# A mixture-of-experts and selective-scan block on one core: expert rooms of 184, 336, 200 and 380 slots, and a job order found with other durations

## The chip, the cores and the metric

The kernel runs on one core of one Trainium2 chip. The metric is device time in microseconds of that core, from start to end of one execution. The core has five engines with programs of their own: PE (TensorE, matrix products and transposes), DVE (VectorE), ACT (ScalarE), POOL (GpSimd) and SP (SyncE, which here issues transfers). Transfers are carried out by 16 DMA engines.

## The reference

The input x has 16×256 tokens of 128 numbers, 4096 tokens in all. Four parts follow each other, each on a layernorm of x and each added to x:

```python
x = x + attn_a(layernorm(x))   # softmax rows sum to 1: in effect one linear map, v then w_out
x = x + ffn(layernorm(x))      # 8 experts, top 2 of a softmax gate
x = x + attn_b(layernorm(x))   # selective scan, 16 states, decaying sums along 256 tokens
x = x + ffn(layernorm(x))      # the same experts once more
...
logits = x @ gate_w;  top_vals, top_idx = top_k(logits, 2);  w = softmax(top_vals)
h = relu(x @ w1[e])            # 128 -> 512
y = h @ w2[e]                  # 512 -> 128
out = sum over the two experts of w * y
```

The reference runs all tokens through all experts and weighs with zeros; the kernel sends a token only to its two experts.

## The kernel before

**Tiling.** The tokens are cut into 8 blocks of 512. Each of the two expert layers treats blocks in sets: `FIRST` (layer 1) is [0], [1], [2,3], [4,5], [6,7]; `SECOND` (layer 2) is [0,1], [2,3], [4,5], [6], [7]. Layer 1 of a set is followed by the scan mixer of its blocks (`arrive`, `mixer`), and layer 2 by the output (`finish`).

**Routing.** For a set, `route` finds each token's two experts and its place in the expert's room, scales the row by the gate's weight, and scatters it to a buffer `slots` in device memory with indirect transfers issued by POOL (4 per block and choice, 128 in all). `experts` then goes over the 8 experts. `collect` gathers each token's two result rows from `ys` (128 indirect transfers of POOL) and adds them to x.

**Rooms.** `SLOTS` gives the slots per expert: its first tuple is for layer 1, its second for layer 2, and within each the first number is for sets of one block and the second for sets of two. `divided` rounds a room to nc chunks of np partitions: nc is the room over 128, rounded up, and np the room over nc, rounded up. So 192 is 2×96, 330 is 3×110, 216 is 2×108 and 384 is 3×128. If an expert gets more tokens than its room, a flag that is read at the end runs the whole of `general()`.

**One expert pass** (`experts`, N slots as C chunks of K partitions): a fetch `xs<-slots` (SP, K partitions × C rows of 512 bytes, strided in device memory by the 8 experts), C transposes on PE, an eviction `xsT`, four products with `w1` (128×N each), relu into `h`, four products with `w2` into `ps_y`, an eviction `yT`, C transposes, an eviction `yr`, and a store `ys<-yr` on SP. There are 80 passes, and so 80 fetches and 80 stores: 16 passes of 192 slots, 24 of 330, 24 of 384, 16 of 216. The tiles xs and yr have four buffers each. The fetch and the store are

```python
x = new("xs", [P, CMAX, P], bufs=XS)[0:K, 0:C]
move(x, q.part(q.slots, e, i), 4 * N * P, turn="fetch")
...
move(q.part(q.ys, e, i), yr, 4 * N * P, key=f"out{q.name}")
...
v = t[NE * i * self.n : NE * (i + 1) * self.n]
return v.rearrange("(p c e) w -> e p c w", e=NE, c=self.nc)[e]
```

**The mixer** treats a block in 8 steps of two states each. A step has two pairs of PE products that spread the states' rows over partitions (`ps_B`, `ps_C`), exponentials and tanh on ACT, and on DVE a product, a scan of 1024 elements (`w`) and two more products; pairs of steps are added (`th`, on DVE or POOL) and go through PE into `ps_s`.

**What sets the order.** Nothing is issued while the program is written down: every operation becomes a job of `Plan` with a duration from `cost` (line 712; matmuls in line 780, transfers in `move`), the tiles it needs and the jobs it follows. `forward` builds a schedule: it takes, again and again, the job that can start earliest, and among equals the one with the better rank; jobs that `either` lists with several engines (PSUM evictions, some additions) go to the one that starts first. The ranks are decoded from the string `ORDER`. The program is then written in order of these starts, so that each engine's program, SP's and POOL's among them, is fixed; on the chip each engine runs its program in that order. All jobs are recorded under line 710 of the profile; scatters are line 807, gathers line 821.

Of the kernel before, what the change touches and what calls it, by code (L numbers as in the profile page):

```python
# [40 lines left out]
XN, ROW, XS, XT, H, YT, DEPTH = 4, 3, 4, 3, 4, 3, 3  # L41

ORDER = (
    "c-oy;3zS?{m92a3_kHWtzxw}AcS6!hI-~;z$O;57;6V8Q2_u0S5d^_uSc)<WMU9}iM3yW-9GO9x!6gH;R9KFnMgszpL;?f?f"
    "k*<R^Xq@t@4Y*x(n)u9Rdv$gbywAU_uY5jJ?HGR&pu3!7%XbbZAPKv1@3dL7-PWr9y>~ce89&%(C@K%Jo9!(hVu?i`7ck&TU"
    "=}!eF%Vl)_8eOGlzoV+GCP40*uyj))&`!j{^V`L0}L96gZ<4gs;O)2b>A*3(6>rA1qHftKE)g1PD&+d4C53zj>tYtuRmST4)"
    "&WZ=i;-Wdt8&k}Jkz4frZfW0dx>2F9<qDP7bBq>YMzaZlQu8;l;?+ePSH#x<oKoEc04YdQ9_z#2UcR8YkQZ@_JKUIwrXpCBw"
    "y%n$|z+H*Fet87`^C*_nH1fcC_oYqiEa5-i%s&Llw`v@46X#t7>ItB=v6B`tD>z8D<E*H}0f-#>loAIJY14hsV+|<5QxV>F6"
    ">MACb|KehA*xQaiirRK`r;~{cLjneDt0Nf|kEoo*U@p9_j!i#dWsezvrR+sxshv)zuWsGhFh-7pml~U+|6RMg#e{BnBi1OJ8"
    "{AtKz1A~GTIhQXQRn%ke_1+;3-()<bWZJRR6xkpvtH^UoJyCT1TFBd-vKZw{l=N5^8I7n;k;oMd;@Ct0ds)?$Q&UmPXz}F6#"  # L50
    "dW9?-*SWOvxor10@uUMTT|4)h($^?t#9+p%<8@UwC4u_H&;{uTgXsAMiMbl@4dSA0RXZ4ACKM^vhG!qIZ3nF^_^|>`d-Tn&K"
    "wyzk<LlLQRB1Sh~zY_bopU;AF}%AS(s#+{Wm8iwK;{49U2`nGz1AY|+UEUrmJ%G;LyF9NZ`WH88wyQ>luGWVmKT3OV<!#{EW"
    "z!NIr5>A!W@A}UR$AWI|yFk+BEncN=R!(&QNPwlz&?wY>(L5$Xj@WkfMZ5@g#l8cWfdX#yell3CZhJqETdv4Sl?uKS~-)v})"
    "*4Vd22ckBKk|8VVy=0BLVS=}uE1S@ZYfgCSgm>u8<lgqPqc<;kc?rNJurWMKMhvbR2qEm+|2UcJKs<96Vvpuj0d3D4Ol{~jD"
    "cbd9cbIWM858=Cz7YhCRBII%{;(YO>*0hKYgrutqLc+%P%RBi3%*?jzD0>I3<3Efd@<bwI+I<3KauaD-H2gE37^e)@TEs7Rl"
    "mCTe(M@e{Hq2=o>!CxJnq#en9mpN*lS+&Iw2j!+`ts4{f2PVMHH#yYYq^BZsi=|-|t8(JfC6;{iqKJpA{YQK>8{db}Y7%1%m"
    "$WPD1#pR5Rju3=MF*JyEdPx|=W?&I655)808;G9f7ezWWA3XfwvOg@aHMUvd&5l5TnkS>p^$u;L$4aYP5jbo}#ADG_H0DKuj"
    "u!Z7tjkurLfov96nM^nzTX@8{Q$937vRW0C-5uOb^Oj3%l#B4<#!j~c5E#e_fwC;J+RCpwK|NPft1JPleU~<FVRNIdf6eaz_"
    "Nv0P>Z+A!CEICH}&6*u~1??PyUf7eg8@uY%b;<r%k|>f-k1T$sZg1Me)YxXVdWNeW?%8tuHdp{3#ogBbYA;w0bivzZvubm=S"
    ";u|tWYNdXxF6B#=HHK)3%~O5?RK;+SsOX+qgTI%sagY#bZ33c{lh?fXeo(UeK9XlQ!l>}&R7jB33OpT{afUf*+^D_6L!6*c<"  # L60
    "h7L9m@!!-^s_fy|QfmDvDt?3h}Vp{*$OLDcCS%nsc8svmPfsu)&;TDFcKF;EU}a@<8*34~xXDg|A}%sHpKTeo9dE`>kiXNE!"
    "2}Rao~0CdHr>Vh5vv;!0oyH0!d8k45OvgXmyL7+J<Yl^FG(U|O>XL3Z^p+mWlK0Gj2vl>bFE98-Xh<|d<ttXm_ycw_46$d*="
    "N{H*TW<G$1MvHzy|X*oCAKl|_DUET4E2{EZ~6~SV(+hdkJ2eiw&E}+CZo)u}D7<-j8X)h}#*5`2TRY(d%ak`I(om3YX7XQ;-"
    "82r-(aOFxjFT(DFH3&d<{WUmyg<*(gK;*T8E51PH6`c5O%$++arQY0k=N}_YL3^ZMXC|Hk8Tkp7kug{EMoc)KVA>SNEd*jOR"
    "9YC!pixRCZz|TuC8>TjE2Sd2j>|k}_jex`*77FX%xVN5;iP64HL+aT94Q(>1jRGe9_6W#Uzmtbw}b7x^s&|tS_9HVKCt5A<r"
    ";K3#2~{Q$LJJ~Hs`_xjttq@*ZSwWyjf2SC@AZj@tRoMK)SD!2#kI>vgzGf`??{<_J?ayD>|GN-@g6sACYC`O>cGby6Yag{&{"
    "i}+$XP#SP|(-qF~Kw%fXLgv}ls@Vcf(y{7%z2MX{bU?!9o?c~7re&u%04nm5av&iTz*iXBTg#+qYc$6S5>Z_diGZg@Lf6Z@l"
    ")wW4G;Y_;oS5sUq}{^J@BankP?#tvB!n0-i|(&S41wf@8QeqzI@v|6^xKn>E_@SbQwN(5yWll87$l4ZQ+dV~^R$DnXlPzYRo"
    ")nh#23O4sr7AdIyNKVav-OU8V&iXsz8B^JL-v%twpAwQ=Qp|pL-T}0+fY4v3M`J_Ct2}NOAeM^U#$*H;)v^arT5v56Py~LZy"
    "KtG#Z#A8=wV{w6{Aq2UK4;F$;&&I4XD{lhb2fGEE&R*a#-{EVssn+QktixhOrgXABzgXo6auRe$x$=KXq4BsUH~Xp{8b1kln"  # L70
    "N+6lChLhmik8mt@M}Y;tMZR#K=n$X_u5IpFss8+P{mW+v!LiI0f_TD5d!MEHHWJ{fMhI2>AeM8WT~lFC&MDJMTtfyM<#FVQG"
    "6lvYlzEg5Xy?ijwILJC0%|7jEaAdM4HQ9Ul^>ZtxO2d*7_vQ`_~SaB^+CfzpN?51RLemBMwz*BO@dmSRRDbMiV)Q)90R8v)z"
    "PHZ9pW?~U#))Iqb7HGfO(OYbK0V2jtFoI3HtT9vb*jfliR`xD_|=fpUst#pJqUfuD|?7`1i9dy4PmcQ6C_ua2TI`NL#X@*mg"
    "FRefEuh)`e$Qz<7@yzC)%_k#wz7<VN(?nT?jN!h38#$$@B&A}fNhKD)_V3C>6?W_Km;UG4d2i226s4(^Prc~oj9DzqGETcK8"
    "l1I%Z`po^mmqr`!`l4Z+3U}RBpKnhl}a~$D~2#N!gR!o$meVKHLX;2^h2XY87cFhMkAv)*fxxquK9mk7i_+QICRJ`ksSbxqM"
    "*I8qi^KK9B8|S>`kad*b*wWhc}`O7B-;)d)e~yQKVGI!z@(HG(2T0$>Pb^WShXEOR;`2lv#Y9kQb>_Ogj2i=fq_yU67CeVZr"
    "{@gsGEVbJj_oU$d>DPTCh!;?-g}h~-P|d6M0v5E0K_4$xYQ1gxnot`W$KR~PH@`L`l|7UC;<sTQxWUQ6||poTy22!i!IhKzy"
    "pXQf3l-Gg!A-@Dv~rsY^rO)gVE@UZZmD)VdP0}msHuac5QY{JGYJL#qvpHEjmiedOSa1F&HY|ulVc)O@cHts`I{@eiBjwR(!"
    "_8ix^k!l0(h~&T7vM4e5KVN*DYOK3E+dhbWdb3?O^7)&A1eAW?=7Vz!2K8hi*_g1DL}BPd81oY)3j%rzwa6$#het4-Ihzya7"
    "77H$j6raj9Caxc6jsy)rla2BZ#kLR!ussM?-TivyE_K=-%6eQ%Dy}IKPmF8KGQE(BPY{&sD0aUkypJowK$5&pz3Zxld!;r4b"  # L80
    "i{@8#QJ_IFn*;{VzcdLVpURg@j=$V-dy;p8g9$&<0E*5r}RnW4ssP!0vkwhv!q5M?mqtJQ-&7z$ANdJr>3`CNU5J!(3K065A"
    "i+L-$}&JeEnTAef=kA}-sw&-e>J#HChX&52<yMomPBiDcydpfxkF<esn+mybj<nYg@AEfou;>8oatI$$gl&*zUTVA&_w=>d0"
    ")VuxalN-e>{1?hHd#T<gEY603Sq;ya#Gqh_Mm3NVtcv12paWEAp@N;jl_QKli;?LCjg<s`!{TB$IU6ISyA=LpWVI7x57}ZFu"
    "UyR@ii5A&vj>Y+kR=nMcOp1blceu7K&ZmLJKbnmXE#R8F_*sih9<z#X+;A%6{A{Ez$^$XzqzsgPamGSd;v$zQUxv|TBU}pJO"
    "amc?{~0On8j*%t>`(S5uz_(gF0ig2eO`~@C)l`YfsL7i$mXvUPy{QQMzyN>t{N*$*BV(<B)RH{Zi?qJ-47zZD6A6QTNl6PX5"
    "ISpC}NRp5Pnd{WL_F(JZ&*EA26kJwh%tbQBz`jL{MqK*a1OmW2Y&=;)dCIpY+M<9hn6WW0SGk%=for-_rsND|HXUrYeDY^Wt"
    "uRc9iXm1sqF%8mqwdiz%BgB3yFq0D1xK{)d$SD=|z!!`R#$kn*RmVr&^uNvVT^94rO$#9JszL!=M5ANyV03eex*#vqAJ5%Ny"
    "4jqAju=(&N=4uCL$VU#40LZNbPG?#1NILG;DwkqZqSz2uCi;rN@$1`Lu><|JJbQm8p-oY1<G0KV!2gME%*-8+W+2sVI7iO}V"
    "by#4#`*ZG+D5_>`9E(B_QH4OGPsRbTmB)28Dj{m%J|AhKbS}aVhfpCwQ3T%8MPLEt0_hZ!m=-&iwY`GPJ764^K~`KA)|>;ZT"
    "@}ro$BSFRTs>(OgIUG3@gF-FYys&tR|0K7L5=Q1R;Acpqk2X^1mlt)<4r;#9V#Ar;xBaY8bA8LwH`k|bnD=W9={Cqp~?6mho"  # L90
    "&4_Wy<Nnt3%6`4o`d?Jc7`~W)6IU(A0xWeYE66moHm&C{%Swf1)8>zM4L0V)e(guDC4q`lQj5u0A+aaZ8un3Qd1Ymv1sxdPR"
    "bXpF`2ny4=hvZmZ(jB1TFvQ!y*3d@871G&uZwjyQCLcvtak_0a06QK|H{u2@M=iF$eXLNf~A_>t8mIX5}CBwCXxTAHI}2I<h"
    "`E~}xkx}PS^I0)w{z$;7M(mMgE@bH1*P=z1LhC|cMJ}fL|GOVkadMHZ|Iwe#A`toNgp%6N%#M5OoJ7Xx|oBi^Al<r1{j)cBY"
    "l~?L1sL<2Fxe}N<G+K_!DGWB1<tAJ`9fwY^rJe?ox=L6Hjs_FgT9+F+bp=uascEUaWHugt_1Qsn0t`Y``6H-EgwhO|E(3LFi"
    "Z?4fSLUZ9QdC9!r$s_l{2aE7_!YHqVmIU{%F`z!%!=I%kKZ5%&Cmzc%b~}~q>IM!rb81tqy!K!VUCYqq#7$!!==bhCX=3s;$"
    "%^*;wCa3OO-O9o(ZQ-hqNQio)L;mia^O(WxDCmOmSION~THP!{KuJTjQtx^z2P$M2bgM$Pd4pP-rZqEAXmI7_yZA^bv5zLiv"
    "(<9@0~Uc6m5-C3WfQIGd(iPb1aJH#rlw)TN|RU9cU3796-NOrQ-8{Em$WuY$d&)W2z2U6(ZvewlXCrKM0GRTY^=ugp-!=%Y&"
    "Fsu8My`l0<!hGyKW_?@eYMLo3~SMyobTC68?dK%$h)m{3q^-@n)MyH}zA67bsj(WIKz)be3x{NFe<qcAG^{A`%9Fy8f&&*3R"
# [1408 lines left out]
```

## Time and profile before

| | |
|---|---|
| median of 9 runs | 724.56 us (719.81 to 727.77) |
| profiled execution, its own time | 724.92 us |
| its span | 723.2 us |
| mean granted clock of PE | 0.916 |
| busy: PE / DVE / ACT / POOL | 624.1 / 554.4 / 487.9 / 414.7 us |
| first expert matmul / first scan | 50 / 128.4 us |
| expert matmuls of 192 slots | 57 to 131 us |
| of 330 slots | 137 to 388 us |
| of 384 slots | 398 to 638.9 us |
| of 216 slots | 641.6 to 698.2 us |
| last scan ends | 622.7 us |

The profile is of one execution. Busy time is given per engine, and a matmul in four-byte floats appears as two records. "PEclk" is the clock that was granted to PE, as a share of its full speed. Windows give, for a stretch of time, the busy time of each engine in it (with the number of instructions), the granted clock, the mean busy share of the 16 DMA engines and the bytes moved. The table of waits sums up, for each engine and operation, the idle time ahead of it by what ended it. "SPq" is SP's sequencer issuing transfers. From 700 us on only the tail is left: the last stores, gathers, one addition, transposes, a copy and the output transfer.

### The profile page before, as it was taken

To read this page: it belongs to the slowest core of one execution; us is meant where nothing else is said; L and a number is where in the kernel's file an instruction comes from. 1 tells how busy PE (TensorE), PEld (TensorE's weight loads), DVE (VectorE), ACT (ScalarE), POOL (GpSimd) and SP (SyncE) were. 2 spreads that over 40 slices of the span, in tenths; PEclk is the share of its full clock that TensorE was granted. 3 is DMA by queue.
4 is the path that set the end of the run, shared out by engine and by line. 5 is a ranking of instruction groups with operands and counts; after the bars stand their busy time and mean duration, and the time that the engine had idled before them with its cause. 6 is when DMAs were issued, how large, how long until landed. Compare 5 with 4: busy or idle time off the path is not lost. (4 is left out here: it accounts for less than half of the span.)

```text
span 723.2 us, 8786 instructions
## 1 busy us (share of the span) xinstructions
PE 624.1 (86%) x2598; PEld 390.2 (54%) x2598; DVE 554.4 (77%) x1038; ACT 487.9 (67%) x996; POOL 414.7 (57%) x490
## 2 busy tenths in 40 slices
PE   5478999799999769899898889887999999999971
PEld 4366877465645226555344554333555455578860
DVE  4765448999998798899999898998988998740120
ACT  2243538988967797679989678788877775355440
POOL 5367771496075458677954852864037787324743
PEclk8557999999999889799999999889999999999995
DMA  8931331211330001421123210210112512213342
GB/s 229 339 111 52 95 99 42 72 54 47 88 87 19 1 30 46 117 61 37 31 68 82 54 26 30 62 55 23 55 31 79 159 50 69 87 46 104 98 135 76
DMA packets 76373, 55.05 MB, mean 76 GB/s; under 512 B 8064, under 2 KB 69152, under 8 KB 76320
## 3 DMA queue, kind: packets, MB, share of 16 engines
q1 hardware_dynamic: 66464, 37.35, 17.8%
q0 software_dynamic: 8192, 16.79, 8.2%
q10 hardware_dynamic: 1664, 0.29, 0.2%
q8 instruction: 22, 0.36, 0.2%
q14 instruction: 31, 0.25, 0.1%
HBM read 27.09 MB, written 27.32 MB: 75 GB/s over the span
## 5 line engine op out<-in xcount | busy, mean ns | idle before, releaser
L710 PE MATMUL ps_b<-xsT,w_s 128*128 128x330 f32 (+3 forms) x640 | 211.0, 438 | 15.3 <-ACT h L710 6.9
L710 PE MATMUL ps_y<-h,w_s 128*128 128x330 f32 (+3 forms) x640 | 213.7, 424 | 3.4 <-ACT yT L710 2.1
L821 POOL DMA_INDIRECT yy<-ys,of x128 | 124.7, 974 | 100.9 <-DMA ys<-yr 38.4
L807 POOL DMA_INDIRECT slots<-row,to x128 | 126.7, 990 | 79.0 <-issue 22.1
L710 ACT ACTIVATE h<-ps_b 128x384 f32<-128x384 f32 (+2 forms) x234 | 110.2, 476 | 88.5 <-PE ps_b L710 86.1
L710 PEld LDWEIGHTS ps_b<-xsT,w_s 128*128 128x128 f32 x640 | 114.8, 196 | 74.2 <-ACT h L710 24.5
L710 DVE TENSOR_TENSOR_SCAN w<-decay,ps_B 128x1024 f32<-128x1024 f32 x64 | 145.8, 2279 | 0.2
L710 PEld LDWEIGHTS ps_y<-h,w_s 128*128 128x128 f32 x640 | 109.9, 195 | 44.9 <-issue 11.8
L710 ACT ACTIVATE th<-later,lneps,ha_s 128x512 f32<-128x512 f32 x128 | 100.1, 809 | 5.1 <-DVE th L710 2.9
L710 ACT ACTIVATE decay<-delta,nea 128x510 f32<-128x510 f32 x128 | 86.7, 714 | 4.8 <-DVE w L710 3.5
L710 DVE TENSOR_TENSOR ps_B<-du,ps_B 128x1024 f32<-128x1024 f32 x64 | 78.2, 1222 | 13.2 <-PE ps_B L710 13.0
L710 DVE SCALAR_TENSOR_TENSOR ps_C<-th,ps_C 128x1024 f32<-128x1024 f32 x56 | 68.3, 1219 | 7.1 <-PE ps_C L710 7.0
L710 PE MATMUL ps_s<-th,wsh_s 128*128 128x512 f32 x128 | 69.6, 635 | 3.8 <-POOL th L710 3.8
L710 DVE TENSOR_TENSOR th<-ps_C,w 128x1024 f32<-128x1024 f32 x56 | 67.9, 1213 | 0.2
L710 POOL TENSOR_TENSOR th<-th,th 128x1024 f32<-128x1024 f32 x20 | 47.2, 2361 | 29.5 <-DVE th L710 27.1
L710 POOL TENSOR_TENSOR rstd<-var,root 128x8 f32<-128x8 f32 (+1 forms) x20 | 28.2, 1412 | 52.3 <-DVE var L710 49.5
L710 PEld LDWEIGHTS <-sel 96*128 96x128 bf16 x256 | 25.8, 102 | 58.9 <-issue 48.1
L710 PE MATMUL ps_B<-pieces,sel 96*128 96x512 bf16 x128 | 41.5, 397 | 10.2 <-DVE w L710 10.0
L710 PE MATMUL ps_b<-ident,yT 128*110 128x128 f32 (+3 forms) x208 | 43.6, 279 | 3.0 <-ACT h L710 0.8
L710 PE MATMUL ps_b<-ident,xs 110*128 110x110 f32 (+3 forms) x208 | 38.8, 277 | 7.1 <-ACT h L710 3.2
L710 PE MATMUL ps_C<-pieces,sel 96*128 96x512 bf16 x128 | 41.7, 405 | 3.6 <-DVE th L710 3.5
L710 PEld LDWEIGHTS ps_b<-ident,xs 110*128 110x128 f32 (+3 forms) x208 | 26.5, 148 | 26.0 <-ACT h L710 8.5
(161 smaller groups left out, 811.7 us busy)
## 6 DMA issues: line engine op xcount, KB each, us to landing
slots<-blank SPq DMA_DIRECT2D x3, 1536.0 KB
xs<-slots SPq DMA_DIRECT2D x24, 192.0 KB
ys<-yr SPq DMA_DIRECT2D x24, 192.0 KB
w_s<-in_w SPq DMA_DIRECT2D x16, 256.0 KB
xs<-slots SPq DMA_DIRECT2D x24, 165.0 KB
ys<-yr SPq DMA_DIRECT2D x24, 165.0 KB
xT<-in_xT SPq DMA_DIRECT2D x8, 256.0 KB
slots<-row,to POOLq DMA_INDIRECT x128, 2.3
```

What stands on the lines that cost most here:

```text
L710: return lambda: f(*[real(x) for x in a], **{n: real(x) for n, x in k.items()})
L807: inst = nc.gpsimd.indirect_dma_start(out=real(out), out_offset=bass.IndirectOffsetOnAxis(ap=real(rows), axis=0), in_=real(in_), in_offset ...
L821: nc.gpsimd.indirect_dma_start(out=real(out), out_offset=None, in_=real(in_), in_offset=bass.IndirectOffsetOnAxis(ap=real(rows), axis=0), ...
```

## The change

`SLOTS` becomes 184 and 336 for layer 1, 200 and 380 for layer 2. By `divided`, 184 is 2×92, 336 is 3×112, 200 is 2×100, and 380 is rounded up to 381 = 3×127. The duration that the planner takes for a DVE instruction loses its floor of 0.2 us, a scalar operand costs 0.07 instead of 0.08, and `tensor_scalar` and `tensor_copy` between four-byte tiles outside PSUM count half per element; a four-byte matmul counts 1.7 ns a column, at least 0.23 us (0.2 up to 16 columns), where it was 1.78 ns and at least 0.42 (0.25). These durations are only the planner's. `ORDER` is replaced by ranks found with them. A branch is added to the mixer that is taken when ADD equals half the number of states (ADD is 2, NS is 16).

```diff
-SLOTS = ((192, 330, 480, 632), (216, 384, 600, 800))
+SLOTS = ((184, 336, 480, 632), (200, 380, 600, 800))
...
         if engine == "DVE":
-            t = 0.15 + 0.00208 * n if "scan" in name and n > NE else max(0.2, 0.15 + 0.00104 * n)
-            return t + 0.08 * sum(v.free_size() == 1 for v in views[1:] if n > 1)
+            out, *ins = views
+            ins = [v for v in ins if v.free_size() > 1]
+            fast = name in ("tensor_scalar", "tensor_copy") and not any(
+                v.home.psum or v.dtype != F32 for v in (out, *ins)
+            )
+            t = 0.15 + (0.00208 if "scan" in name and n > NE else 0.00052 if fast else 0.00104) * n
+            return t + 0.07 * sum(v.free_size() == 1 for v in views[1:] if n > 1)
...
-        took = max(0.25 if n <= 16 else 0.42, 0.00178 * n) if rhs.dtype == F32 else max(0.06, 0.00044 * n)
+        took = max(0.23 if n > 16 else 0.2, 0.0017 * n) if rhs.dtype == F32 else max(0.06, 0.00044 * n)
...
-            if len(group) == ADD:
+            if len(group) == ADD == NS // 2:
+                product(group[0][:, 0, :], group[0][:, 0, :], group[0][:, 1, :], ALU.add)
+                matmul(so, wsh_s, group[0][:, 0, :], False, True)
+            elif len(group) == ADD:
```

The string `ORDER` is left out here; all of its lines differ.

More of the change, by code (lines that the diff above doesn't have):

```diff
@@ L43 @@
 ORDER = (
[L44 to L98, printed above, removed]
@@ L99 @@
-    "YdmMxAO$n(YeN$ybbOaV6%8^2zS1*j2oGzV{zTp1(Yv#Z&O`qXwp16!"
+    "c-pO333yfInZEz`?`OSx_JjloAp}C$L8?WR2T+SptyXavY9Al1b!=@*TdiXknP=>7Yo|`@Oj~Q~GUGC}wK{_xts76Ps1%Tb)"
+    "Z&H;At7YD_n!05cLF52mzw~c$-|QKpa1;J_r34?y`R^gw-j(L{K4e2jI+GMcv^7rr+3;23yHHOOUVwgKpogzn_I>hrEu5W?k"
+    "X|=;b1<!oPM%U_@8<i2HNumxM1l{2`!8c?u}D0J`rI+WM~DME&$B{Km?&=0bv|~Qd|s&0LN(oB&&TbdIEy)W}UsBk<jvziPv"
+    "jFUQ^w>_j#Phv{VVEgvS_bn1Ns68dL;AFny|Ea_yOfB?%$8GgFKzfR>BSqL9TSa~4QXas^agauy-e7&Vl|m9*$I+<ozNKvI+"
+    "%z(a6GZD8usOBqyfYEcO^?oiDsU-(g=ivd4`G-ozXF~Y0YQ`SIm7Ojs0BM1|<UgNBqpUmuT&vHA++e8$E?L?OaibrDvEKYj_"
@@ new lines @@
+    "2+jv|r4W{2>^Do(y@}t|`W1c3PHaneWeG_`r|+cPWa4fwmmsWy>`P2aJeE%i7iPfLY^_eVz?c18+NBx&PBQI3)gSL!04eD5w"
+    "NSqGtMs9`Pb|_eJ%5id+(5mx$FEH2l&GHo%ye9J?+kGJZMT`ec7eI+R!VKg|L(E{Ucf@lWS3+Dc=cXj7G?}c^b@6vLP1F>I5"
+    "3Xa0gkh*cQ9d;V%(@m?$kLtyYBJCdm>N2y#IyDYafe}%MIn4bFP<2O1IuiiOWRDbrtowx(qY<olW>PmlhL<I!-$%;m<un#9W"
+    "5UQy`WlDi9_s76M-aG^BJAm4eP-!0hv>m`b>y;tGzZ^Y9$>3d-t%X{vKvIkbu}m~k~@Gk|+|Z9FDo1z1~hFyH=8GC$btt2|g"
+    "y=9#A~rKJgoBA}RMlx>Ttf7uDP&t!&oe(F0_`z8!Rmh6vv-p1yFt07K$Y!$yWZm+}ZxI7MBj_Yh4)Pv0=MY>Y<DPBgdzxbYu"
@@ new lines @@
+    "Hi0G}+Qi1wpI)++bdW9fOyy0sKR^G)MemczeAm?F*7dDBr&iIk;pt?%awHcPGok$AFHZ*+^2g3$c)UTUP_Q}8RRlVSBbea8o"
+    "0{@qB1!eXYV*)cQLh_DDi6l_9?}TQHm0GGf@1-X2t_R+k$0Ps7hHz8jt;_9L?7S+|KpNTCVF9rk`(zMY`Kbl*U9IXTvhql3r"
+    "@bU_0irx?v-pnwBPdLpFGk}vmH(6UWuSs8O>&O`k-$qv6clkd+-4U!pF=RX}AU{6Q3c(l6QX<p-|`LT#JXAGgn%_=Y+GR4-w"
+    "2GH#U)$vx-uW&5uZZ-3v$+4=HSfR0WOrnnmzrRac@o%mQvlxtxZ%v}O{*`KCKuLFZ_e;v!@zW-+M%G1vJ;AmRd0Jm8?>65*s"
+    "H)+aNpv!iR`8@&C;O%pbsd9blJnAGWp0~IFKpG3Xm)Z-`_LI;(IKB5I=9gWo9>}nxwB?gShb|?2kA8~D6wKWmQkW|AvDq~g0"
@@ new lines @@
+    "<@0-{6yAqwIF!=%-u`r6BPTmOr!qCi{*pJ~N{nyTf46yCSKF>dkv1d>ndNEcs@}w*`6zpVlh3}^=dmg(NnlxWf@Aw<vXJs8R"
+    "7h%p0JLVhw>g^ea22n#bh<|EbG|$Og?XJsl7iCCE7P}6?;$7yPQA9`{+*Tkt2I=R9;?xR#+kd7(pD6}luEhck)5r(7l8(9C9"
+    "UVS%-(hmB*=hBrYsJR`ngm{CX-#Ml-iNA2dYU1_VJEtw}LSYkZJigS9BoWli&qTjZeE}l|;?G_!qnesnmY&OPIkm6vU2CBzr"
+    ";<&kg=(g7W$Cfm{mge&uQxaaX&4U?!qgDjE{H(H=+?XlT(25pW4MW|~RCl<u@FOCPW>b11Hn-cT9l{!B#Bp6Z|TFETJcNp5L"
+    "cCqt2V{70J?ptvsZ|J(lgTNo!d5eHv~bVm|Xc{>m$CoM+p)p*OO3hncm&(`s<PR?;r+ggO7SgLrKP()5exT>oyLgchc=JmS3"
@@ new lines @@
+    "8XU{Zo)4JHD}N5euW>lS%g`0V1Lt3<VQk%c2J$+Z${?Sny)0qcGUXJ~Z1HYXud^wgcnEc9hLGHyfP9t{E<|v1tQEMaT<j_#1"
+    "g<AGWCsT({vg@QKEBqD=g)bdwtvygCXRF@w5x#>5cG~umBbJgbOZ$zShnpnzx^`Tl3G*w_V3+Xv$wVfP9x9gMVTKq?P+9m8F"
+    "@Of$Wt!Ax#N}jz5EpNygO^c_b0zKvyUu+r`5u%>O5WBu(z(Ccd(b_^yI^CC@bh3veju%EK0^t{pq@&{)lwItBJG4h8w=|xhK"
+    "eS_^m!SYx^QOnXz!~IVc}3C<B1UG?QGJ%G@QD<@<}M`1G0&J-Yg3dNJH1E=X-S?dcEhqaUJwPNx&~p8W8651h~GWb(RhNNp6"
+    "MOv7}tEnQWeaM^7wJE!JI0=gYr@5l@|g1Dql+DWO|GtIl&-z5ps?Rxf>`ZpT}pbFl05?F;8x2Q4lA)8>Z+I9hkGcQOW^dMK("
@@ new lines @@
+    "1;2>b`w5o(-LLIjz$@wAd3WhN7?q<9)$~vh4zL=K0T*#B@wQcS@I2Ijv>%nckG1X!J{T`JaxynzcJXp16cY|k>y?u0UIeLRQ"
+    "B4<?WYBW|nnANzij|WR-R8VE*uhuhed)^%T3yXm_HLDNUc2yIbS8{)q0mh1^|+)zlLg6NJP+y8z_=H3pgq16@p*(~A-9&0%t"
+    "TIT$f$PFoUvP?BK+@PKrGK!j>`KXTj7DycYD2Aw&WtLeX~_z(p$B}-j17~`9bI`y$IFyThu6J8P@G;b@k;cr&#uVT&ZEHN}~"
+    "&*6Qxi*jrU;-)}ffT$jBN2&2g;785D6=Yv=6d*WAHW1<v%F-p=Iv+8&v;J%3ei<(|ofnocadz&>l)&|4ol1(2pvc~XX(w1;8"
+    "&MDu5+{N?N4{QQmhireeOKYsf5YkxqlCqMKqOX`(Q`r3cK=1KS%|FO7IY*_l#8KGXS?n|7n6E#lT>R+vq6I#ieUef*Es%Mra"
@@ new lines @@
+    "i3dS)AU)BmyD{09ttA%Z5`&o?J*nOq2!I~Tb^LUSTbMrjFrlOZcdP+D=w>KSI-8g$sJ@*3vVMUbI@K}@?>nyb2PfxOIE~~D("
+    "c$TN)gL)fv9E(JWY4uFYJb)jx8}lZc!@8x?6~_SYcP@4ZDgBlNj%y3W>Y_DhTUGJYCX$3tL|XMVuk9R?5(=f8T3}uNNEZgja"
+    "CCAY2cPAuh*@BL+>|757aqDNsp1hCkRs(F?qY4&x4&0wZs}=W6_y9F`k-{VDfFOWg6<R{Gt3&6|eFdc5d0oX<>VH{MYBMd=h"
+    "RI;lQ<MivDTto{IDWCHLD_D%n7Y@U#6$29xS*Ks$FXHJsK=!Q8Y8Pa-?`Bq^zQih#{;YQ-=uN5N%IUn|yFpFV`AXE$Afvsa0"
+    "!=-mw8S7TLu_zorGqUS<X&ri*Jk@A|l#>tja^rck4!|%Btp}jtP$dBrBb4JkQ9T5`#xF5^sHI#ImQJ-^WDFmAvmF_?6#yh`f"
@@ new lines @@
+    "=M@oLo~c-hrcjjG-)qS$Zfj`qD;@-*D7;%WVaKAc*B{7z?F)!tV2vJz%z~aY2FS5|MLE(ns72zV`7?$-3o=Ks2A~`S&}7MKf"
+    "eize5+te<Q5L0PDB99e^80MD2pd+X3e!J2dw2M?)?4hyuo|`J^7&TuGuhPC-+X)-5_?jVKkNs(ZNb@J(U<ZY)=&cTZERz-L9"
+    "SRrtcV2QzfjW28eWH86gacA!_)<Y_<Ze7+*Ao8&<n{AOro}$gK9@_-Gl2oLZKxwya_w4L<hQOeq9$Ow2`GEU&b;x%mfw}{%w"
+    "O7nJs9%f*aOr(a0TQ4|U*Xn&p>pn+p-DeTkIEFUKUvZ!Xmbr_A-_={IcV0UmgHOH+T#{q@bcmdg=tlzrAUVT%ckH-yEcL{Ef"
+    "4n}))PM#+SHBPaQJ%;3J1ghFc_IqN7rgOQUDu&t7j?FUt%mG=(~gon5G6?Xmy8h|G^&D``kBH6PWY^w$Brkm_Nu(Afvq);&p"
@@ new lines @@
+    "_7w{2xU_U$@^97So@u;%h;YI#i?eKGO|M_gv$9PNk%kUPRii$@aK>N1fl<T=;e3#D9L%rJLjkXR6^L9QjBC(OzUS!ZSdp2$4"
+    "Ha?~T3Vb2dAtVIxCm+fy(Tn{@syzDUTRnK4$Gn9@h9+rby0qp7AC2+yb}+_tIycdzv96=?sKj{u!R)f%k)U=w=y}fFd{7>FE"
+    "L3}6hYykw?=0Y+6?lF@xUm5BHjS&Gzw`q+HWjPBI^FMj*I$#a}U9(nu`YsH`lzE?61iJAkPbwF6K;P3jwgMhSC~<I8q5skU%"
+    "u>8=D9{joEHg=}=RU!R#Za0Gxp}7XayiW)(lYa4FD**qLF!I@F8e&{<yrT8;UQnm7!qg?~@oKxqoi8CozA^*K1+{z<@=0Ye_"
+    "u8Vnb91+yyigA<+PfQwv4EU*h%RGn};H0a18N&+=B9=SJ;1c0H+#t))JL(oRuAs!oG@J;Ny8{)ciH%4H&>N+$XZ^EN>q90DN"
@@ new lines @@
+    "FIM+80cZ>D7p{RlU?oc3%_{+%p;^^PVZerrUvmzjLqjwgp*Cl5`%H+WQDFE%xwIK^y83j0wkShUPsdmsKSYRP#~f|yqD^230"
+    "(!$jptXo53p)(FaHLe3D9c?cAI67zT@o`UcKFA{%+S9_o{l^m9W&<Wt0TW0{to#yGB-xT!&AbMkA|inUG&JnF+V02D;_t)V~"
+    "3XsOFkgQpB8_90z;;B^Rh#+lb&@<fW}<O6kT;V%EfO-KN=Go=am`jRY_Whe$APYn42Rxi~cK`I(7`k7%`(aG^X5?aLl3D_(L"
+    "a^qvJr}NW6?W26&^WQ1WO_I7g+4C|={3S7jDFyw2e8o5KJxMcFE5m?@@fxjYT;HyTRgMAHn<9Qt#Vx8?aelAW-G1IOn5IB+P"
+    "+zZo-u<<T-a>*1K6nbBb##)65NF}Em@MKda6#Yr87sxdejJGxtuP7FU9QwFv{DMCjcNhyxZSTaz|onlEYhuJcBI6TrvqJfYM"
@@ new lines @@
+    "$FLX!qn;1r(!`Dx!(zk^$J2~o6ppMmlDH#Z5@X6~)@TTZq&!?nkx(8jECDGCf^y(CC30ns2f&bwflE_@%VTO`@zy6RQR9H*<"
+    "i9%nIvBgCoj5MX-SUJ_gK;=SiWV)=LNiMGM(}1#DZXL&0a<tS$(ZBda#$~m1f}T2CjgRB0F3<&05s)in-bK7<xNWwE=}=Gj}"
+    "b3pM$@)fAjiVx2^7KOg2cp19?K|HY&0%Qbiu%Q;2X8pcxG#?gBD+O_?P}sbvG6(7i42js3hYL#PUVTJfeqX6lHYMPoj2~;%o"
+    "$!g|Z@hG~A^y56Z6{jPISJJ098VNPZ7<a3Iq8GCVRP(J*D>R)(zvFKA*VRm2RJsxjCaJD$54!^WDi%f;~)DV=S`9WGNK!eKE"
+    "SD%Xgf;d_qZ5l6iHiD+KTjMC6ipOqlmlyp1Cp1TyH$1kJhde(A>F5a?iK96mC%xH^OR8LGf9+(o<7z5%ZOPbhtO^x|K_o62?"
@@ L100 @@
+    "WJ(*PQJD<OXsj{g@T9ocH>O;3^*3DZ|D{7WW7zu<?;ZPJ!zUZZ"
 )
```

## The prediction

> **What bounds the kernel now.** I read the page from the top: busy shares, then the forty slices, then the queues, and went to the windows and the waits by stage.
>
> ```profile
> span 723.2 us, 8786 instructions
> PE 624.1 (86%) x2598; PEld 390.2 (54%) x2598; DVE 554.4 (77%) x1038; ACT 487.9 (67%) x996; POOL 414.7 (57%) x490
> ...
> PE   5478999799999769899898889887999999999971
> ...
> DVE  4765448999998798899999898998988998740120
> ...
> PEclk8557999999999889799999999889999999999995
> DMA  8931331211330001421123210210112512213342
> ...
> q1 hardware_dynamic: 66464, 37.35, 17.8%
> q0 software_dynamic: 8192, 16.79, 8.2%
> ```
>
> PE is busy for 86% of the span and, but for the start and the last slice, for eight or nine tenths of nearly every slice; DVE goes beside it until the last scan. The DMA row is low: from slice 20 on, the 16 engines are mostly at one to three tenths. The windows by stage agree. From 57 to 128 us PE has 65.59 of 71 us; in 300 to 400 PE has 91.42 and DVE 93.51; in 400 to 500 they have 86.78 and 90.54; from 641 to 700 PE has 57.52 of 59 with DVE at 11.30. So PE bounds the kernel before the first scan (128.4 us) and after the last (622.7 us), and PE and DVE together in between. Among what PE waits for, the longest rows are DVE's x (23.0 us), ACT's h (12.6 us) and the first token load (4.3 us); a slot load (xs<-slots) is not in the list. Transfers are hidden today, in all 80 fetches and 80 stores of expert tiles.
>
> **The change, part by part.**
>
> (1) *Columns on PE.* Slots per expert go 192→184 (16 expert passes), 330→336 (24), 384→381 (24; 380 is rounded up to 3×127) and 216→200 (16). Each pass streams its slots through 8 matmuls: 8×(−8×16 + 6×24 − 3×24 − 16×16) = −2496 columns. Two records of one f32 matmul start 323 ns apart at 384 columns and 278 ns at 330, so a column costs 2×45/54 = 1.67 ns and the sum is −4.2 us; with the transposes of the same rows −4.7 us. By stage: −1.9 before 128 us, +2.1 in the stage of 336, −1.1 in that of 381, −3.8 at the end, where PE is alone and all of it counts.
>
> (2) *Ranks and prices.* The new prices only steer the order and the choice of engine. The changed order has the same 2104 PE matmuls and 202 SP transfers, 21 more DVE instructions (1043→1064) and 15 fewer on ACT (1093→1078). With each kind at its spacing in this trace, DVE's sum rises from 518.9 to 526.1 us: +4.0 before the first scan, 0.1 between first and last scan, +3.1 after it. PE's sum before the first scan's operands rises from 81.1 to 87.7 us, and between them and the last scan falls from 438.4 to 428.2. The larger of the two engines, added over the 63 steps between scans, falls from 499.3 to 494.5 us. What DVE gains at the ends lies beside PE, which has over 57 of 59 us there. So this part is worth about what (1) is, not in addition to it: I take −4.7 for (1) and (2), with ±10 for a list of 4000 jobs that lands differently in time. The branch for groups of NS/2 is never taken (ADD is 2, NS/2 is 8): nothing. No expert gets more tokens than it has room (fullest: 142 of 184, 310 of 336, 318 of 381, 176 of 200, counted from the inputs), so the fallback does not run.
>
> (3) *The transfers of the new tile sizes.* Every fetch and store moves K partitions × C rows of 512 B, and K changes with the slots: 96→92, 110→112, 128→127, 108→100. Here the trace says something that no busy share shows. I counted, for each transfer, the events that its completion adds to its semaphore. A fetch or store of 96 or 128 partitions has 16 events, all at its landing. One of 110 has one event 1.2 us after issue and 11 at the landing; one of 108 has one early and 12 at the landing. 11 and 12 are the largest numbers up to 16 that divide 110 and 108. The transfer rates say the same:
>
> ```profile
> 431.95:432.76 0.81, 0.81 (x4) 0.39 (x3) 0.81 (x6) 0.81 (x3) 0.00 (x0) 1.00 0.86 243
> ...
> 290.33:291.45 1.12, 1.12 (x7) 0.69 (x6) 1.09 (x2) 0.58 (x1) 0.90 (x3) 1.00 0.58 150
> 383.85:384.97 1.12, 0.95 (x7) 0.44 (x5) 1.12 (x5) 1.12 (x3) 1.02 (x1) 1.00 0.58 150
> 133.44:134.00 0.56, 0.00 (x0) 0.00 (x0) 0.56 (x2) 0.56 (x3) 0.00 (x0) 1.00 0.70 175
> ```
>
> Each window is one transfer alone; the last two columns are the share of the 16 engines and GB/s. 384 rows take 0.81 us at 243 GB/s; 330 rows, fewer bytes, take 1.12 us at 150 GB/s, with a share (0.58) below 11/16. Their median issue-to-landing times are 2.91 us (fetch of 384) and 3.21 us (fetch of 330).
>
> Carried on: 92 partitions have 4 as the largest divisor up to 16, 112 have 16, 100 have 10, and 127, a prime, has 1. A move of 381 rows would then go through one engine, one row after the other.
>
> The price of a row on one engine: the median packet of 512 B takes 27 ns (over 60,000 of them). 24 passes × 2 moves × 381 rows = 18,288 rows; × 27 ns = 494 us, if it is always the same engine. To it come that engine's part of everything else: queue q0 takes 8.2% of 723.2 us on each engine, 59 us, of which about a third falls into this stage, 20 us. So 514 us of one engine's time, where the stage has, from the issue of the first 384-row fetch (369.6 us) to the last matmul of its experts (638.9 us), 269 us. Nothing covers the difference: PE's order has the mixer's jobs of the next blocks between these experts, and waits with them.
>
> Two ends of the sum. If the last group (200 slots) is computed while the last stores of 381 rows still drain, the end comes 514 us after 369.6 plus the 60.3 us that now lie between the last 384-row store's issue (662.9) and the end: 369.6 + 514 + 60.3 = 944. If nothing overlaps, the whole stage grows by 514 − 269 = 245 and the rest loses 3 to 5: 965. I take 955 us.
>
> The ns per row, bounded from both sides: from 192 to 384 rows the window grows by 0.25 us for 12 rows an engine, 21 ns (381 us for all; end near 831); the 330-row window has 1.12 us for 30 rows an engine, 37 ns (677 us; end near 1127); the issue-to-landing difference of 96 and 110 partitions, 0.76 us for 18 rows, would be 42 ns (768 us; near 1218). I stay with 27, the median of single packets, since a long queue leaves no latency in the sum; the fill of the slots, 3584 rows seen in 5.59 us, gives 25 ns per row and engine.
>
> The other sizes: 184 rows on 4 engines are 46 rows, 1.2 us instead of 0.3, and land about 1 us later, with 4 buffers to hide it; 336 on 16 gains 0.4 us a move; 200 on 10 engines has 20 rows an engine, as 216 on 12 has 18. All three I cost at nothing to 2 us; the cover is the fetch made ahead into four buffers.
>
> [...]
>
> **Rivals.**
>
> (a) *One engine a move, but another one each time.* Then moves overlap on different engines and only latency grows: 381×27 ns = 10.3 us a move, some 9.5 later than now. Passes come every 10 us (240.8 us for 24) and four buffers let fetches run some 30 us ahead. Exposed is the first fetch of each of three groups, which waits for its scatters (SP's waits for those: 62.9 us in 9), 3×9.5 = 28 at most, less where mixer work covers: about +12, near 735. For it: nothing in the trace shows which engines are taken. Against it: the 0.58 share of the 330-row moves shows no overlap of neighbours.
>
> (b) *Not slower: the divisor does not rule at 127.* The engines share 381 rows as 16 uneven parts (24 rows at most, as for 384). Then only (1) and (2) count: 724.9 − 4.7 = 720, and the sign hangs on whether the reordering keeps its ±10. It decides if the first 127-partition fetch lands within 3 us. Against it: 108 and 110 partitions were not shared unevenly, though 14 engines of 8 would have served 110 nearly as well.
>
> (c) *The replanned order stalls* with all transfers as now: a late scatter or a full PSUM bank costs 5 to 15 us, near 735. PE already waits 23.0 us for DVE's x.
>
> **How the numbers follow.** The forecast, one engine for all 381-row moves: 0.85, near 955. (a) 0.08, near 735. (b) 0.05, near 720. (c) 0.02. The sum is made on the profiled execution (724.92 us, span 723.2), 0.4 above the median of the runs (724.56), which is less than the terms can resolve. The range, 850 to 1150, takes the bounds of 22 to 37 ns a row; about 0.04 of the forecast's cases and all of (a) to (c) lie outside, 0.19 together. A measurement of this kernel can tell about 0.5% from no change; faster by more than that is most of (b), 0.04; within it 0.03, from (b) and (c); slower 0.93.
>
> **What would show it.** Right: fetches and stores of 127 partitions with 15 early events and one at the landing, landing 10 us and more after issue, queued ones far more; a DMA share near 1/16 (0.06 to 0.12) from about 370 to 880 us; PE's waits headed by slot loads, or by ACT and DVE work behind them; the granted clock at half where PE idles; the stages of 184, 336 and 200 within some us of before. Wrong: 16 events at the landing of 127-partition moves and fetches landing under 4 us would fell (3) and leave (1) and (2); 10 us landings without a queue would be (a). If landings are slow but the stage ends near 800, the row price is below 21 ns.

## The result and the profile after

The changed kernel takes 977.83 us (median of 10 runs, 972.86 to 982.98) against 725.38 us (31 runs), a ratio of 1.348 (95% interval 1.344 to 1.352). The profiled execution has a span of 976.7 us and a mean granted clock of 0.826 (before 0.916).

The page of the kernel after, the same rows as were shown of the kernel before, and the chain of work that ended last:

```profile
span 976.7 us, 8807 instructions
...
PE 645.9 (66%) x2598; PEld 400.9 (41%) x2598; DVE 559.7 (57%) x1059; ACT 483.9 (50%) x981; POOL 411.1 (42%) x489
...
PE   4679999889879876555976490609503781449791
...
PEclk9569999999989987867998795859855886679996
DMA  8722322020113100112010000011100000211332
...
q1 hardware_dynamic: 64912, 37.03, 13.2%
...
PE 40%; DMA 23%; DVE 10%; ACT 8%; issue 5%; POOL 5%; SPq 4%; POOLq 0%; DVEq 0%; ACTq 0%
```

Busy times hardly moved (DVE by 5 us, PE by 22); the share of PE fell from 86% to 66%. From about 390 us on (the 17th slice) PE's row has holes that were not there, and just there the DMA row shows mostly zeros and ones. Read alone, that row says that the transfers have nothing to do. The last line contradicts it: 23% of the chain that ended last are transfers. A low share of 16 engines alone does not tell an idle queue from one engine that never stops.

What PE waited for, in us, times and longest:

```profile
PE ps_b L710 <- DMA xs<-slots: 110.8, 11, 42.6
PE ps_C L710 <- DVE th L710: 53.1, 10, 33.0
```

In the kernel before, the first of these rows was

```profile
PE ps_b L710 <- DMA xs<-slots: 0.2, 1, 0.2
```

The prediction says that a slot load is not in the list of what PE waits for; it is, with these 0.2 us. Two stretches inside the stage of 381 slots:

```profile
570.00:580.00 10.00, 9.54 (x37) 5.73 (x37) 8.66 (x18) 9.29 (x17) 0.00 (x0) 1.00 0.08 20
...
727.00:737.00 10.00, 0.00 (x0) 0.00 (x0) 0.00 (x0) 0.00 (x0) 0.00 (x0) 0.50 0.07 21
```

A line has start and end, length, busy us and instructions of PE, PEld, DVE, ACT and POOL, granted clock, DMA share and GB/s. In the second stretch all engines stand still for 10 us, the granted clock is at half, and the transfers move 21 GB/s at a share of 0.07, near 1/16. One move lands in that time, at 730.5 us.

The completion events of the 127-partition moves: one early, and one at the landing. A move issued to an empty queue lands about 12 us after issue (11.7 to 12.5); over all 24 of each kind the median is 23.0 us for fetches and 20.9 for stores, most of it spent behind others. Queued fetches land 9.86 us apart (median of 22), stores 8.98 us (20). The moves of 92, 112 and 100 partitions have 4, 16 and 10 events at the landing, as carried on in the prediction.

### The profile page after: what moved, and what is told of

Its sections match the earlier page's. It is cut to its first block, busy times and chain, and to the rows that moved or that the text cites. A ratio compares the mean times of both kernels' runs of the same rounds, so it can differ in the third digit from the quotient of the medians.

```text
span 976.7 us, 8807 instructions
## 1 busy us (share of the span) xinstructions
PE 645.9 (66%) x2598; PEld 400.9 (41%) x2598; DVE 559.7 (57%) x1059; ACT 483.9 (50%) x981; POOL 411.1 (42%) x489
## 4 chain that ended last, share of the span: by engine, by line
PE 40%; DMA 23%; DVE 10%; ACT 8%; issue 5%; POOL 5%; SPq 4%; POOLq 0%; DVEq 0%; ACTq 0%
PE ps_b L710 22%; DMA xs<-slots 12%; PE ps_y L710 11%; DMA ys<-yr 9%; PE ps_s L710 4%; SPq L710 4%; POOL yy L826 4%; DVE w L710 3%; DMA yy<-ys,of 2%; DVE th L710 2%; ACT decay L710 2%; PE ps_C L710 2%; PE ps_B L710 1%; ACT h L710 1%; ACT th L710 1%
## 5 line engine op out<-in xcount | busy, mean ns | idle before, releaser
L710 PE MATMUL ps_b<-xsT,w_s 128*128 128x336 f32 (+3 forms) x640 | 218.1, 455 | 74.9 <-DVE h L710 33.7
L710 PE MATMUL ps_y<-h,w_s 128*128 128x336 f32 (+3 forms) x640 | 217.3, 435 | 5.7 <-ACT yT L710 5.4
L710 ACT ACTIVATE h<-ps_b 128x336 f32<-128x336 f32 (+3 forms) x234 | 109.6, 472 | 145.6 <-PE ps_b L710 142.2
L710 PEld LDWEIGHTS ps_b<-xsT,w_s 128*128 128x128 f32 x640 | 120.4, 208 | 141.4 <-DVE h L710 34.5
L710 PE MATMUL ps_b<-ident,xs 112*128 112x112 f32 (+3 forms) x208 | 42.0, 293 | 115.9 <-DMA xs<-slots 110.8
L710 POOL TENSOR_TENSOR th<-th,th 128x1024 f32<-128x1024 f32 x23 | 54.1, 2356 | 86.7 <-PE ps_b L710 34.5
L710 ACT COPY xsT<-ps_b 128x336 f32<-128x336 f32 (+3 forms) x63 | 26.2, 418 | 121.2 <-PE ps_b L710 120.5
L710 PEld LDWEIGHTS ps_b<-ident,xs 112*128 112x128 f32 (+3 forms) x208 | 28.0, 155 | 137.9 <-issue 118.0
L710 DVE TENSOR_SCALAR h<-ps_b 128x381 f32<-128x381 f32 (+3 forms) x22 | 11.8, 537 | 91.2 <-PE ps_b L710 91.0
L710 DVE TENSOR_TENSOR x<-x,yy 128x512 f32<-128x512 f32 x16 | 12.7, 794 | 69.9 <-DMA yy<-ys,of 69.8
```

Source lines behind the costliest of these rows:

```text
L710: return lambda: f(*[real(x) for x in a], **{n: real(x) for n, x in k.items()})
```

## The experiments

In most runs the order is held: every engine's program is, instruction by instruction, that of the kernel named, only sizes differ. To that end the planner is given the durations of the sizes it had (`PLANNED` maps new sizes to those; in the last experiment `LAYERED` does so, with one map for each layer):

```diff
+    def planned(v):
+        n = v.free_size()
+        if tuple(v.shape) == (P, n):
+            return PLANNED.get(n, n)
...
-        n = rhs.free_size()
+        n = planned(rhs)
...
-            late=-float(size), **order,
+            late=-float(4 * P * PLANNED.get(size // (4 * P), size // (4 * P))), **order,
```

### Back to 384 slots, in the new order

```diff
-SLOTS = ((184, 336, 480, 632), (200, 380, 600, 800))
+SLOTS = ((184, 336, 480, 632), (200, 384, 600, 800))
+    PLANNED = {384: 381}
```

> The changed kernel with 384 slots (3x128) in place of 381, every engine's program in the very order of the changed kernel. Theory (381-row moves over one DMA engine are the cost): the 16 engines come back, 720 to 745 us; the upper end is because the profile after is already 18 us late when the first 127-partition fetch is issued, which that theory does not explain. Rival (the new order or the other rooms stall): stays above 900 us.

Measured 738.01 us, ratio 1.019 (1.015 to 1.022). Three more slots an expert, 240 us less. The stage, by windows of 100 us:

```profile
400.00:500.00 100.00, 87.40 (x287) 42.21 (x288) 90.95 (x119) 78.48 (x149) 66.37 (x62) 0.89 0.17 48
500.00:600.00 100.00, 98.14 (x378) 55.21 (x377) 91.32 (x135) 76.39 (x153) 51.19 (x59) 1.00 0.24 68
```

From 500 to 600 us PE is at 98 of 100 us again. But 13.5 us over the kernel before remain.

### Only 380, in the old order

```diff
-SLOTS = ((192, 330, 480, 632), (216, 384, 600, 800))
+SLOTS = ((192, 330, 480, 632), (216, 380, 600, 800))
+    PLANNED = {381: 384}
```

> The kernel before with 381 slots (3x127) in place of 384 alone, its order kept. Theory (one engine): 24 passes x 2 moves x 381 rows x 26 ns = 475 us of one engine, so 940 to 980 us. Rival (the new order stalls): 720 to 740 us, since nothing but 3 slots an expert is changed.

Measured 941.91 us, ratio 1.301 (1.296 to 1.306). That one number of the change costs 217 us by itself in the old order, and 240 in the new.

### The same 127 partitions, moved as 112 and 15

```diff
+        if size == 4 * 381 * P:
+            parts = [call(e.dma_start, (), dict(out=out[s], in_=in_[s])) for s in (slice(0, 112), slice(112, 127))]
+            emit = lambda: [f() for f in parts]
```

> The changed kernel, its order and its 381 slots kept, but each fetch and store of 127 partitions issued as two, of 112 and of 15 partitions (16 and 15 as largest divisors). Theory (one engine): 722 to 750 us, 48 more issues on SP of 0.7 us each included. Rival (127 partitions or 381 slots are slow by themselves on PE, or the order stalls): above 900 us.

Measured 734.42 us, ratio 1.015 (1.010 to 1.020), with 48 transfers more, in the order of the changed kernel. The fetch of 112 lands after 2.71 us (median, all 48 of that size), that of 15 after 2.40. This is no slower than the 738.01 us with 384 slots. So 127 partitions cost nothing on PE or in SBUF (the on-chip memory of the tiles); carrying them in one transfer does.

### 118 partitions: two engines

```diff
-SLOTS = ((184, 336, 480, 632), (200, 380, 600, 800))
+SLOTS = ((184, 336, 480, 632), (200, 354, 600, 800))
+    PLANNED = {354: 381}
```

> The changed kernel with 354 slots (3x118, largest divisor 2) in place of 381, its order kept. Theory (the number of engines is the largest divisor up to 16): moves land after some 6 us with 2 completions, one engine has 48 x 177 rows x 26 ns = 221 us in a stage of some 250 to 270: 735 to 800 us. Rival (only one engine each, the prime 127 or not): 48 x 354 x 26 ns = 442 us, 930 to 960. Rival (16 engines except at 127): below 735, and landings near 3 us.

Measured 795.70 us, ratio 1.099 (1.092 to 1.106). The moves have two events at their landing; queued ones land 4.58 us (fetches) and 4.19 us (stores) apart, half of what 127 partitions take. While one queued fetch was carried out:

```profile
507.61:512.18 4.57, 2.98 (x10) 0.75 (x8) 4.41 (x6) 4.51 (x7) 0.78 (x2) 1.00 0.14 40
```

The share is 0.14, near 2/16, and the rate 40 GB/s, twice that of 127 partitions.

### 113 partitions: one engine, fewer rows

```diff
-SLOTS = ((184, 336, 480, 632), (200, 380, 600, 800))
+SLOTS = ((184, 336, 480, 632), (200, 339, 600, 800))
+    PLANNED = {339: 381}
```

> The changed kernel's order with 339 slots (3x113, 113 a prime) in place of 381. Theory (one engine, time per row): 48 x 42 rows fewer at 24 to 26 ns are 48 to 52 us off 978, 925 to 932 us. Rival (a fixed price for a one-engine move): unchanged but for PE's columns, 42 x 8 x 24 x 1.67 ns = 13 us which are not on the path, 965 to 978 us.

Measured 935.92 us (two runs), ratio 1.291 (1.286 to 1.297): 42 us less than with 381, where 48 to 52 were expected and the fixed price gave at most 13. The time during which a move was under way (from its first event to its landing, overlaps counted once), over the rows, is nearly the same in three runs: 474.3 us for 18,288 rows (381) is 25.9 ns; 423.4 us for 16,272 (339) is 26.0 ns; 230.9 us for 8,496 rows an engine (354, two engines) is 27.2 ns. So the moves do take 51 us less. The 42 differ from that because the time without any of these moves under way, from the first issue to the last landing, grew from 54.6 to 64.5 us.

### Stores on another queue

```diff
         e = dict(SP=nc.sync, ACT=nc.scalar)[engine]
+        if order.get("key", "").startswith("out") and size == 4 * 381 * P:
+            e = nc.scalar
```

> The changed kernel in its order, but the 24 stores of 381 rows are issued by ACT's queue instead of SP's; the fetches stay on SP's. Theory (every 127-partition move goes to the same one engine, whoever issues it): the engine has the same 48 x 381 rows, so no gain: 960 to 1010 us, the upper part if ACT is held at its issues as SP was (up to 11.3 us each). Rival (each queue has an engine of its own, so fetches and stores overlap): half the rows an engine, 229 us, as in the run with 118 partitions, 780 to 860 us.

Measured 1040.66 us. The chip of this run is slower: the kernel before took 793.46 us on it (7 runs), a ratio of 1.306 (1.296 to 1.317). Neither number can be held against the expected 960 to 1010 us, because the transfers are not slower with the chip: fetches that had the engine to themselves landed 9.8 to 9.9 us apart here too. Both lie far above the rival's 860 (1.306 times 724.56 us is 947). The stage itself, from the first fetch's issue to the last landing, took 541 us, and 529 in the changed kernel: no gain. The landings show why (us from the span's start, fetches on SP's queue, stores on ACT's):

```
fetches  782.8  800.7  817.2  835.1  853.1  867.9
stores   790.8  808.7  828.2  846.1  864.1
```

With both queues busy each lands a move about every 18 us (14.8 to 19.5), in turn; with one queue busy it was 9.86 and 8.98. One fetch and one store after the other take 9.86 + 8.98 = 18.8 us on one queue, so on two queues they share one engine here too. SP's issues show it as well, kernel after first, then this one:

```profile
547.60 39.35 SPq L710 DMA_DIRECT2D xs<-slots  x4
```

```profile
742.58 86.78 SPq L710 DMA_DIRECT2D xs<-slots  x6
```

(start, duration in all, number of issues): 9.8 us an issue in the first, 14.5 in the second.

### The new order alone

```diff
-SLOTS = ((184, 336, 480, 632), (200, 380, 600, 800))
+SLOTS = ((192, 330, 480, 632), (216, 384, 600, 800))
+    PLANNED = {192: 184, 330: 336, 216: 200, 384: 381}
```

> The rooms of the kernel before (192, 330, 216, 384) in the very order of the changed kernel: the new ranks alone. The prediction's step (2) put them at about nothing: 715 to 730 us. The theory formed after the same-order run at 384 slots (738.0 us, first scan 9 us late): the new order loses the 13 us by itself, mostly before the first scan, where PE is busy 30 us of the first 57 instead of 34: 735 to 745 us.

Measured 739.11 us, ratio 1.019 (1.015 to 1.023). The order alone costs 13.7 us. The first scan starts at 140.9 us (128.4 before), that of block 4 at 387.6 (370.4), the last at 631.0 (620.5), and the span is 14.1 longer. One place in the head can be read off. PE around the first expert, in the new order (start, duration, operation, in brackets the idle time before it):

```profile
55.31 1.97 PE L710 MATMUL ps_b<-ident,xT 128*128 128x128 f32 x8 [0.59 <-ACT x L710]
57.10 2.07 PE L710 MATMUL ps_b<-wat,xT 128*128 128x128 f32 x8
58.97 1.01 PE L710 MATMUL ps_b<-ident,xT 128*128 128x128 f32 x4
60.65 0.39 PE L710 MATMUL ps_b<-ident,xs 96*128 96x96 f32 x2 [0.68 <-ACT x L710]
```

and in the kernel before:

```profile
50.28 2.08 PE L710 MATMUL ps_b<-wat,xT 128*128 128x128 f32 x8
...
52.99 0.66 PE L710 MATMUL ps_b<-ident,xT 128*128 128x128 f32 x4 [0.33 <-DVE rank L710]
54.33 0.38 PE L710 MATMUL ps_b<-ident,xs 96*128 96x96 f32 x2 [0.68 <-ACT x L710]
```

The first fetch landed at 53.9 us in the new order, and its transposes (ident,xs) start at 60.65: twenty PE records on xT, the attention's input, stand ahead of them. Before, it landed at 51.1 and the transposes start at 54.33. Here alone 3.5 us more pass between landing and use; that all of them reach the first scan, which is 12.5 us late, is not shown.

### The new rooms alone, without 127

```diff
-SLOTS = ((192, 330, 480, 632), (216, 384, 600, 800))
+SLOTS = ((184, 336, 480, 632), (200, 384, 600, 800))
+    PLANNED = {184: 192, 336: 330, 200: 216}
```

> The order of the kernel before, with rooms of 184, 336, 200 and 384 (transfers over 4, 16, 10 and 16 engines): the rooms without the 127-partition moves. The prediction's step (1): minus 1920 PE columns, minus 3.2 us, so 718 to 724 us. The rival (transfers over 4 and 10 engines are late for PE): 728 to 740 us.

Measured 727.26 us (11 runs) beside 725.39 (15), ratio 1.002 (0.999 to 1.005). The 3.2 us that the columns should bring did not come, and transfers over 4 and 10 engines do no visible harm.

### 192 in place of 184, new order

```diff
-SLOTS = ((184, 336, 480, 632), (200, 380, 600, 800))
+SLOTS = ((192, 336, 480, 632), (200, 384, 600, 800))
+    PLANNED = {192: 184, 384: 381}
```

> The changed kernel's order with 192 and 384 slots in place of 184 and 381: against the same-order run with 184 (738.0 us) it puts the fetches and stores of the first two sets back from 4 to 16 engines, for 1.7 us more of PE columns. Theory (landing 0.6 us later is covered by four buffers): 737 to 741 us. Rival (4 engines cost the late start): 725 to 732 us.

Measured 736.55 us, ratio 1.017 (1.014 to 1.020), beside 1.019 with 184: no difference that these runs can tell. The four-engine transfers are not what makes the new order late.

### Old ranks with new prices, and the reverse

The first takes the changed kernel with the old `ORDER` and the old `SLOTS`, the second the kernel before with the new `ORDER` (the strings themselves are left out):

```diff
-SLOTS = ((184, 336, 480, 632), (200, 380, 600, 800))
+SLOTS = ((192, 330, 480, 632), (216, 384, 600, 800))
...
-ORDER = (new ranks)
+ORDER = (old ranks)
```

```diff
-ORDER = (old ranks)
+ORDER = (new ranks)
```

> The ranks and rooms of the kernel before, with the planner's new prices. Which of the two makes the new order 13.7 us slower? If the prices do: 735 to 745 us. If the ranks do, and prices only nudge the order: 722 to 731 us.

> The new ranks with the old prices and old rooms. If the ranks make the new order slow: 733 to 750 us. If the prices do: 722 to 731 us.

Measured 738.45 us, ratio 1.018 (1.012 to 1.023), and 740.09 us, ratio 1.019 (1.013 to 1.024). My question had no single answer: each half of the change costs the 13 us by itself, and both together cost no more. The old ranks are good only with the old prices.

The profiles of the slower orders agree on the place. In the kernel before, 521 PE records with 99.35 us of PE's time lie ahead of the first scan, at 128.4 us. With the new order and 384 slots they are 571 (103.96 us, scan at 137.6), with the new order and the old rooms 571 (105.56 us, at 140.9), with the old ranks and new prices 562 (108.44 us, at 141.5), with the new ranks and old prices 569 (109.15 us, at 142.7). From the start of the first scan to that of the last, all five take 490 to 496 us. So the loss lies mostly ahead of the first scan, and a half to two thirds of that loss is PE work that stood behind that scan before. This is read from the profiles; no run moved that work alone, and the rest was not isolated.

### Chunks in multiples of 16 partitions, fewest columns

```diff
-SLOTS = ((192, 330, 480, 632), (216, 384, 600, 800))
+SLOTS = ((160, 336, 480, 632), (192, 336, 600, 800))
+    LAYERED = (None, {160: 192, 336: 330}, {192: 216, 336: 384})
```

> The kernel before in its own order, with rooms whose chunks are multiples of 16 partitions and as small as these tokens allow: 160 (2x80), 336 (3x112) in layer 1; 192 (2x96), 336 (3x112) in layer 2. All moves on 16 engines. PE columns: 8 x (-32x16 + 6x24 - 48x24 - 24x16) = -15232, at 1.67 ns 25 us. Theory (first and last stage count in full, 6.8 and 5.1 us, the steps between scans by about half): 705 to 712 us. Rival (DVE holds the middle, fewer columns only widen PE's waits): 712 to 718 us.

Measured 725.06 us (11 runs, 717.15 to 728.79) beside 726.06 (15 runs), ratio 0.996 (0.992 to 1.000). Both expectations missed: 25 us of columns bring at most some 6. A possible reason shows in the clock. The windows of the profiled execution, which is the longest of the eleven (728.79 us):

```profile
57.00:128.00 71.00, 64.10 (x368) 53.19 (x366) 38.48 (x167) 35.47 (x94) 41.89 (x58) 0.87 0.24 68
...
400.00:500.00 100.00, 87.60 (x292) 46.42 (x293) 90.33 (x119) 76.19 (x149) 62.37 (x60) 0.86 0.16 44
```

and those of the kernel before:

```profile
57.00:128.00 71.00, 65.59 (x364) 53.56 (x364) 40.57 (x163) 38.52 (x95) 40.69 (x58) 0.94 0.26 73
...
400.00:500.00 100.00, 86.78 (x292) 43.03 (x291) 90.54 (x118) 77.59 (x146) 62.76 (x59) 0.91 0.15 44
```

A product of 160 columns stands 138 ns from record to record at full clock where one of 192 stands 165: the columns are saved. But the granted clock is 0.87 beside 0.94 and 0.86 beside 0.91, and PE is about as long busy as before. Time at half clock is 155.0 us in this profile and 123.3 in that of before. Since this is the longest execution, its windows overstate the difference: over all runs the mean clock is 0.909 (median of 11, 0.895 in the profiled one) and 0.921 (15). That fewer columns lower the clock, and which part of the missing 20 us this is, was not settled; DVE, at 90 of 100 us in the second window of both kernels, is a second possible reason.

## Why the prediction was right, and where it was off

**The transfers (3).** One engine for 127 partitions was the case, by the events, the share of 0.07, by two edits that undo it (384 slots, the split), one that halves it (354) and one that leaves it with fewer rows (339). What was forecast as 15 early events appears as one, as with 108 and 110 partitions in the kernel before (about 1.2 us after issue there). The events at the landing are 16 for 96, 112 and 128 partitions, 12 for 108, 11 for 110, 10 for 100, 4 for 92, 2 for 118 and 1 for 127: at each of these nine sizes the largest divisor up to 16, as (3) carried it on. That all moves of 127 partitions go through the same engine was an assumption of the sum ("if it is always the same engine"). Landings 9.86 and 8.98 us apart on one queue, and about 18 us apart on each of two, fit it; the engine's number is not in the trace.

**The sum.** The lower end of the forecast was 369.6 + 514 + 60.3 = 944. In the profile the first fetch of the stage is issued at 394.3, the last store at 911.6, and the end comes 65.1 after that: 394.3 + 517.3 + 65.1 = 976.7. So the stage itself was met within 4 us, but by terms that cancel. The moves were under way for 474 us, where 494 for rows and 20 for scatters and gathers had been added up. From 394.3 to the last landing (923.2) there are 55 us without any of these moves under way, which the sum did not have. The scatters and gathers (queue q0) do show: of 41 moves issued well ahead of the landing before theirs, the 30 without any of q0's packets beside them followed that landing by at most 0.01 us more than the medians of 9.86 and 8.98 us, and the 11 with some by 0.4 to 1.5 us more, 10 us in all. By the medians a row of a fetch takes 25.9 ns and one of a store 23.6, and not 27. The overlap of the last group's work with the last stores was seen (its loads are issued from 863.7 on), so the lower end was the better form. Of the 32.7 us above it, 24.7 are the late start of the stage. That 955 came within 2.4% of 977.83 us is thus in part luck: the mechanism was right, and errors in its terms offset each other. In the old order, where the start is not late, 380 slots gave 941.91 us beside 944.

**Steps (1) and (2), −4.7 ± 10 us, were wrong.** The late start belongs to them. The order costs 13.7 us, and with it the first 384-row fetch is issued at 394.3 us with the old rooms too; the rooms without 127 cost nothing that can be measured, and the 3.2 us of columns did not come. The sum that (2) rests on, "The larger of the two engines, added over the 63 steps between scans, falls from 499.3 to 494.5 us", is not contradicted: from the start of the first scan to that of the last the new order takes 490.1 us and the old one 492.1. The step that failed is that this sum starts at the first scan. (2) lists 6.6 us more of PE's work ahead of that scan's operands (81.1 to 87.7), in a stretch that it says PE bounds, and counts nothing for it. The profiles show 6.2 us more of PE's time there and the first scan 12.5 us later. A sum of durations per engine also does not see a job that is ready behind others in its engine's program, as the first expert's transposes are. Rival (c) priced a stall of the new order at 5 to 15 us, as an alternative to (3); a loss of that size came in addition to it. That its causes, a late scatter or a full PSUM bank, were at work is not shown.

**Rivals.** (a), another engine each time, falls with the landings one after the other on one queue (9.86 and 8.98 us apart) and in turn on two (about 18 us on each). (b), 16 uneven shares, falls with landings 11.7 to 12.5 us after issue to an empty queue. The forecast's low price for 184 and 200 slots held (ratio 1.002 with the new rooms without 127, and no difference between 184 and 192).

## What to carry to other kernels

Before a tile's partition count is trimmed, look at its divisors: here a transfer of 127 partitions ran at a DMA share of 0.07 to 0.08, near 1/16, one of 113 took the same time a row (26.0 ns beside 25.9), and the kernel took 977.83 and 935.92 us with them; three more rows (128 partitions, 738.01 us) or a second transfer (734.42 us) were far cheaper. In a profile, read the DMA share against 1/16 and 2/16 (0.07 to 0.08 and 0.14 here), and count a transfer's completions; here a low share beside engines that waited for loads was a transfer on few engines. A list of ranks and the planner's durations act together: the old ranks lost 13 us when only the durations changed, and the new ranks lost as much with either durations, although the sums of busy time between the scans had looked better. Add up the work ahead of the first scan as well, where one engine bounds.
